# A value queue that may empty three chunks, earlier reads for endings, and shift rows begun two half steps sooner

## The chip, the cores and the metric

The kernel runs on one core of a Trainium2 chip. The metric is the device time of one execution in microseconds; the time before is the median of three runs, 5637.28 us (5630.33 to 5653.89). The profile is one more execution, taken by the hardware profiler.

## The reference

The input x has 8 batch items of 2048 tokens with 512 channels, all in float32. The layer computes

```
xn = layernorm(x)
q, k = xn @ Wq.T + bq, xn @ Wk.T + bk          # 8 heads of 8 channels
v    = xn @ Wv.T + bv                           # 8 heads of 64 channels
scores = q k^T / sqrt(8);  scores = where(scores >= 0, scores, 0.2 * scores)
s   = gamma * (softmax(scores) @ v) + xn
ffn = xn @ W.T + sum_e gate_e * (xn @ Wd_e.T @ Wu_e.T)   # 4 experts of rank 1, 2, 4, 8;
                                                # only the top gate of a token is kept
out = x + s * silu(ffn)
```

The gate is a softmax over scaled cosines between a projection of xn (Wp, bp) and `sim`.

## The kernel before

**The attention loop.** A batch item has 4 blocks of 512 tokens and 4 pairs of heads. A *sequence* is one (item b, pair p, query block n), so there are 16 sequences in an item and 128 in all; sequence s has pair s % 4 and block (s % 16) // 4 (`where`, L524). A sequence goes over the 2048 keys in 16 *chunks* of 128. The inner loop of the main program (L1030 to L1057) takes one chunk per pass; I call a pass a *half step*, as the code's helpers do, and i is its chunk. A half step issues, in this order: the shift of the current scores by their row maximum as a matmul of two rows (`less_max`, L657), the score matmuls of the next chunk (`score`, L640), one maximum unit of a later sequence (`max_unit`: matmuls mx, L586, and a VectorE maximum mxr, L597), the exponentials on ScalarE (`exp`, L669), the leaky slope of the next scores on ScalarE (`leaky`, L651), then a filler, and the addition of the exponentials on GpSimd for the denominators (`add_up`, L701, 128 x 1024 elements; none at i = 0).

**Maxima.** The softmax subtracts the true row maximum, so the maxima of a sequence are computed one sequence ahead. The unit of half step i of sequence s is number s*16 + i + 16 + LEAD, with LEAD = 9; the first 16 + LEAD units are done in the prologue. All units share one PSUM tile with one buffer (`ps_x`), so the matmuls of a unit wait for the VectorE maximum of the unit before. When the last unit of a sequence has been issued (at i = 6), `shift_rows` (L599) is put into slot 1 of a small scheduler.

**The scheduler.** There are three slots: an *ending* of a sequence, a `shift_rows`, and the background work `behind` (projections of the next item, `project_block`, and the feed-forward part of this one, `lift_block`). Each is a generator whose yields say how it may be continued. `go_on` (L810), called first in every filler, advances slots that said IDLE, so one IDLE is one half step. The filler is `half_full` (L833) for items 0 to 6 and `half_light` for the last. It either issues *values*, that is the matmuls `weigh` (av, L681) of one or two chunks waiting in the list `last`, or background matmuls, by a budget `due`. `run` counts how many chunks of values a half step may take, at most two and not past the end of a sequence; a chunk that ends a sequence and stands first is `alone`.

**shift_rows.** First half step: a reduction m (L603, VectorE). Next: big and max (L609, L610, VectorE), and six small GpSimd instructions (L611 to L616), which stand ahead of that half step's addition. After two IDLEs: a 32 x 32 transpose (L621, VectorE), four DMAs that write it to SH (L623) and four that read SH back into the tile shift (L629). All DMAs are issued by SyncE, in order.

**Ending.** The values of the last chunk put `ending` (L703) into slot 0. It copies the sums avs from PSUM (L708); in the next half step it waits until its block has been lifted, then reads gs, xs[:,0] and xs[:,1] (L714 to L717, 256 KB each: gated feed-forward, x, and xn from HBM); after three more IDLEs come the denominators (matmuls L724; VectorE L732, L734, L736), in the next half step the transposes atp (L741; VectorE L743, L744, the latter reads xs), and in the one after L747 and L748, followed by the write of the output. The tile that L741 to L748 use is in PSUM pool `ps_m`, of one buffer, as are most tiles of the background. On TensorE and VectorE all of this stands in program order with the scores and maxima.

Of the kernel before, what the change touches and what calls it, by code (L numbers as in the profile page):

```python
# [8 lines left out]
FP = mybir.dt.float32  # L9
# [12 lines left out]
NT = BLK // 128  # L22
# [10 lines left out]
def fused_layer_kernel(  # L33
# [37 lines left out]
    nc = tc.nc  # L71
    B, M, C = x.shape
    NC = C // 128
    NB = M // BLK
    CH = NB * NT
    SEQ = NPAIR * NB

    xv = x.rearrange("b (n p t) c -> b n p t c", p=128, t=NT)
# [5 lines left out]
    two = ctx.enter_context(tc.tile_pool(name="two", bufs=2))  # L84
# [12 lines left out]
    GS = [tc.dram_tile([NB, 128, NT, C], FP, name=f"GS{b}") for b in range(B)]  # L97
    XN = [tc.dram_tile([NB, 128, NT, C], FP, name=f"XN{b}") for b in range(B)]
# [145 lines left out]
    TINY, SLOW, WAIT, HOLD, FREE, IDLE = 5, 4, 3, 2, 1, 0  # L244
# [50 lines left out]
    lifted = []  # L295
# [228 lines left out]
    def where(s):  # L524
        return s // SEQ, s % NPAIR, (s % SEQ) // NPAIR
# [28 lines left out]
    def load_values(s):  # L554
        if s >= B * SEQ:
            return
        b, p, n = where(s)
        while b not in valued:
            force()
        vts[s] = two.tile([128, CH, 128], FP, name="v_sb")  # L560
        nc.sync.dma_start(out=vts[s], in_=VS[b][p])
# [37 lines left out]
    def shift_rows(s):  # L599
        if s >= B * SEQ:  # L600
            return
        m = sm.tile([128, 2 * NT, 1], FP, name="m")
        nc.vector.reduce_max(m, mxr.pop(s).rearrange("p e t n -> p (e t) n"), axis=AX.X)  # L603
        yield IDLE

        ml = sm.tile([128, 2 * NT], FP, name="ml")
        c = parts[s % 2][:, 0 : 4 * NT].rearrange("p (i m) -> p i m", i=2)
        big = sm.tile([128, 2 * NT], FP, name="big")
        nc.vector.tensor_scalar(big, m[:, :, 0], 0.0, SLOPE, ALU.min, ALU.mult)  # L609
        nc.vector.tensor_scalar_max(m[:, :, 0], m[:, :, 0], 0.0)  # L610
        nc.gpsimd.tensor_tensor(ml, m[:, :, 0], big, ALU.add)  # L611
        nc.gpsimd.tensor_tensor(big, ml, splitter.to_broadcast([128, 2 * NT]), ALU.mult)
        nc.gpsimd.tensor_tensor(ml, ml, minus_one.to_broadcast([128, 2 * NT]), ALU.mult)
        nc.gpsimd.tensor_tensor(c[:, 1, :], big, ml, ALU.subtract)
        nc.gpsimd.tensor_tensor(c[:, 0, :], big, c[:, 1, :], ALU.subtract)
        nc.gpsimd.tensor_tensor(c[:, 1, :], ml, c[:, 0, :], ALU.subtract)  # L616
        for _ in range(2):
            yield IDLE

        cT = sm.tile([128, 32], FP, name="cT")  # L620
        nc.vector.transpose(cT, parts[s % 2])  # L621
        for q in range(4):
            nc.sync.dma_start(  # L623
                out=SH[s % 2][:, :, :, q, :].rearrange("i e t j -> (i e t) j"),
                in_=cT[32 * q : 32 * q + 4 * NT, :],
            )
        shift = qp.tile([128, BLK], FR, name="shift")
        for g in range(4):
            nc.sync.dma_start(  # L629
                out=shift[STK * g : STK * g + 2, :].bitcast(FP),  # L630
                in_=SH[s % 2][:, g % 2].rearrange("i t q j -> i (t q j)"),
            )
        shifts[s] = shift
# [59 lines left out]
    def add_up(s, i, ex):  # L693
# [6 lines left out]
            acc[s] = two.tile([128, 2, BLK], FP, name="acc")  # L700
        nc.gpsimd.tensor_tensor(acc[s], old, ex, ALU.add)  # L701

    def ending(s):  # L703

        b, p, n = where(s)
        cols = slice(p * 128, (p + 1) * 128)
        avs = two.tile([128, BLK], FP, name="avs")
        nc.vector.tensor_copy(avs, avt.pop(s))  # L708
        yield IDLE
        sums = acc.pop(s)  # L710
        while (b, n) not in lifted:
            yield IDLE
        gs = two.tile([128, NT, 128], FP, name="gs")
        nc.sync.dma_start(out=gs, in_=GS[b][n][:, :, cols])  # L714
        xs = two.tile([128, 2, NT, 128], FP, name="xs")
        nc.sync.dma_start(out=xs[:, 0], in_=xv[b, n][:, :, cols])
        nc.sync.dma_start(out=xs[:, 1], in_=XN[b][n][:, :, cols])  # L717
        for _ in range(3):
            yield IDLE
        yield TINY  # L720

        dps = ps_m.tile([128, 2, NT, 32], FP, name="dps2", tag="m")
        for q in range(4):
            nc.tensor.matmul(  # L724
                dps[32 * q : 32 * q + 32],
                lhsT=ones[:, 0:32],
                rhs=sums.rearrange("p e (t q j) -> p e t q j", t=NT, q=4)[:, :, :, q, :],
                start=True,
                stop=True,
            )  # L730
        dv = dps.rearrange("p e t j -> p (e t) j")
        nc.vector.tensor_tensor(dv, dv, diag.unsqueeze(1).to_broadcast([128, 2 * NT, 32]), ALU.mult)  # L732
        rd = sm.tile([128, NT, 2, 1], FP, name="rd")
        nc.vector.reduce_sum(rd.rearrange("p t e o -> p e t o"), dps, axis=AX.X)  # L734
        rd = rd.rearrange("p t e o -> p (t e) o")
        nc.vector.reciprocal(rd, rd)  # L736
        spend(0.5)
        yield TINY
        tp = ps_m.tile([128, NT, 128], FP, name="atp", tag="m")
        for t in range(NT):  # L740
            nc.tensor.transpose(tp[:, t, :], avs[:, t * 128 : (t + 1) * 128], ident)  # L741
        tv = tp.rearrange("p t (e d) -> p (t e) d", e=2)
        nc.vector.tensor_tensor(tv, tv, rd.to_broadcast([128, NT * 2, DV]), ALU.mult)  # L743
        nc.vector.tensor_tensor(tp, tp, xs[:, 1], ALU.add)  # L744
        spend(0.5)
        yield WAIT
        nc.vector.tensor_tensor(tp, tp, gs, ALU.mult)  # L747
        nc.vector.tensor_tensor(gs, tp, xs[:, 0], ALU.add)  # L748
        nc.sync.dma_start(out=ov[b, n][:, :, cols], in_=gs)
# [5 lines left out]
    for b in range(B):  # L755
# [7 lines left out]
        t0, run = SEQ * b + LIFTED, 0.0  # L763
# [11 lines left out]
    def due_at(h):  # L775
        w, t = h * END, 0.0
        for _, _, _, cost, end in tasks:
            w += cost * max(0.0, min(1.0, (h - t) / (end - t)))
            t = end
        return w  # L780
# [44 lines left out]
    last = []  # L825
# [7 lines left out]
    def half_full():  # L833


        run = 0
        for w in last[:2]:
            run += 1
            if w[1] == CH - 1:
                break  # L840
        alone = run and last[0][1] == CH - 1
        if go_on():
            values(run)
            return
        j = (ahead() or [None])[0]
        if j == 2 and state[2] != HOLD and spent[0] > due[0] + AHEAD:
            j = None
        if j is not None and state[j] == TINY:
            values(min(run, 1))
            go(j)  # L850
            ended[0] = True
        elif j is None or len(last) > MUCH - (state[j] != HOLD) or (ended[0] and run > 1):
            ended[0] = False
            for g in stats.values():
                next(g, None)
            values(run)
        else:
            if alone:
                values(1)
            go(j)  # L860
            if state[j] == HOLD and not alone:
                go(j)
            ended[0] = state[j] != HOLD
# [15 lines left out]

    MUCH, AHEAD = 3, 6.0  # L880

    LEAD = 9
    END = 1.0
    total = B * SEQ * CH

    with tc.manual_schedule():
# [110 lines left out]
        first, late = shift_rows(0), set_up_ffn(ul)  # L997
        units = [(0, u) for u in range(CH)] + [(1, u) for u in range(LEAD)]
        for n in range(1, NB):
# [30 lines left out]
        for s in range(B * SEQ):  # L1030
            for i in range(CH):
                if i <= 3 and s + 2 not in qst and (where(s + 2)[0] in (0, *ready) or i == 3):
                    load_stacks(s + 2)
                if i >= 6 and s + 1 not in vts and (where(s + 1)[0] in valued or i == 13):
                    load_values(s + 1)
                due[0] = due_at(s + (i + 1) / CH)
                u = s * CH + i + CH + LEAD
                nxt = s * CH + i + 1


                less_max(s, i, sc0, 0)
                if nxt < total:
                    sc1 = score(nxt // CH, nxt % CH)
                max_unit(u // CH, u % CH, flip=True)
                less_max(s, i, sc0, 1)
                if u % CH == CH - 1 and u < total:
                    queue[1], state[1] = shift_rows(u // CH), IDLE
                ex = exp(sc0)
                if nxt < total:
                    leaky(sc1)  # L1050
                if s < (B - 1) * SEQ:
                    half_full()
                else:
                    half_light()
                add_up(s, i, ex)
                last.append((s, i, ex))
                sc0 = sc1  # L1057
# [47 lines left out]
```

## Time and profile before

| | |
|---|---|
| median of three runs | 5637.28 us (5630.33 to 5653.89) |
| profiled execution | 5619.18 us, its span 5617.4 us |
| TensorE / VectorE / ScalarE / GpSimd busy | 96% / 65% / 79% / 85% |
| mean granted TensorE clock | 0.968 |
| instructions | 78032 |
| big, L609 | 128 times, 51.3 us, mean 401 ns |
| GpSimd additions, L701 | 1792 times with two inputs, mean 2361 ns |

The page gives the busy time of each engine and its share of the span, then groups of instructions by line; a group line names the source line, the engine, the operation, the tiles (out <- in), the count, the busy time and mean length, then the idle time of the engine before them and who ended it. An entry `A <- B` in the waits says that engine and line A stood still until B had finished. Matmuls of float32 appear as two records each. Weight loads (PEld) overlap matmuls, so their waits count only if TensorE's matmuls (PE) stop too. The granted clock is 1 or 0.5 in this trace.

### The profile page before, as it was taken

To read this page: it belongs to the slowest core of one execution; us is meant where nothing else is said; L and a number is where in the kernel's file an instruction comes from. 1 tells how busy PE (TensorE), PEld (TensorE's weight loads), DVE (VectorE), ACT (ScalarE), POOL (GpSimd) and SP (SyncE) were. 2 spreads that over 40 slices of the span, in tenths; PEclk is the share of its full clock that TensorE was granted. 3 is DMA by queue.
4 is the path that set the end of the run, shared out by engine and by line. 5 is a ranking of instruction groups with operands and counts; after the bars stand their busy time and mean duration, and the time that the engine had idled before them with its cause. 6 is when DMAs were issued, how large, how long until landed. Compare 5 with 4: busy or idle time off the path is not lost.

```text
span 5617.4 us, 78032 instructions
## 1 busy us (share of the span) xinstructions
PE 5378.9 (96%) x26258; PEld 1999.1 (36%) x26258; DVE 3673.9 (65%) x4988; ACT 4440.7 (79%) x8627; POOL 4779.1 (85%) x2906
## 2 busy tenths in 40 slices
PE   8999999999999999999999999999999999999998
PEld 3333333333333333333333333333333333333332
DVE  5577666766676666667666666666766766645653
ACT  2788878888888878888788887888878888767777
POOL 1789988888888888888888888888888888878878
PEclk9999999999999999999999999999999999979989
DMA  5333432434324343252432434234343333322221
GB/s 197 106 112 121 128 113 88 128 106 147 104 78 142 93 146 95 76 158 91 142 92 83 147 112 130 80 111 131 107 123 99 102 120 122 100 78 78 71 63 61
DMA packets 528264, 615.38 MB, mean 110 GB/s; under 512 B 44092, under 2 KB 438332, under 8 KB 491768
## 3 DMA queue, kind: packets, MB, share of 16 engines
q1 hardware_dynamic: 527864, 610.39, 35.6%
q8 instruction: 209, 3.42, 0.3%
q14 instruction: 191, 1.56, 0.1%
HBM read 407.88 MB, written 202.38 MB: 109 GB/s over the span
## 4 chain that ended last, share of the span: by engine, by line
PE 80%; ACT 8%; DVE 7%; DMA 2%; issue 2%; SPq 1%; POOL 1%; POOLq 0%; ACTq 0%; DVEq 0%
PE av L681 28%; PE sc L657 16%; PE zps L279 9%; PE vps L279 8%; PE mx L586 7%; ACT ex L669 5%; ACT sc L651 2%; PE pps L265 2%; DVE mxr L597 2%; PE qkps L265 2%; PE dps L265 2%; PE dps L724 1%; DMA xs<-XN 1%; PE atp L741 1%; DVE gs L748 1%
## 5 line engine op out<-in xcount | busy, mean ns | idle before, releaser
L701 POOL TENSOR_TENSOR acc<-acc,ex 128x1024 f32<-128x1024 f32 x1792 | 4231.0, 2361 | 301.7 <-ACT ex L669 189.3
L597 DVE TENSOR_REDUCE mxr<-mx 128x2 f32<-128x1024 f32 x2032 | 2480.2, 1221 | 1260.0 <-PE sc L657 1018.5
L669 ACT ACTIVATE ex<-sc 128x512 f32<-128x512 f32 x4096 | 2231.0, 597 | 972.2 <-PE sc L657 829.0
L651 ACT ACTIVATE sc<-sc 128x512 f32<-128x512 f32 x4096 | 2237.7, 593 | 18.9 <-PE sc L640 18.9
L681 PE MATMUL av<-ex,v_sb 128*64 128x512 f32 x8192 | 2149.5, 630 | 11.6 <-DVE avs L708 9.2
L657 PE MATMUL sc<-shift,ones_r 2*128 2x512 f32 x4096 | 1679.7, 463 | 75.5 <-ACT sc L651 66.9
L586 PE MATMUL mx<-k,q_sb 32*128 32x512 f32 x4096 | 1445.4, 454 | 37.0 <-DVE mxr L597 35.9
L657 PEld LDWEIGHTS sc<-shift,ones_r 2*128 2x128 f32 x4096 | 703.6, 187 | 1560.4 <-ACT sc L651 1450.5
L640 PE MATMUL sc<-q_sb,k 32*128 32x512 f32 x4096 | 1037.4, 503 | 0.0
L681 PEld LDWEIGHTS av<-ex,v_sb 128*64 128x64 f32 x8192 | 469.7, 138 | 839.6 <-issue 805.2
L586 PEld LDWEIGHTS mx<-k,q_sb 32*128 32x128 f32 x4096 | 562.2, 188 | 61.2 <-DVE mxr L597 49.4
L279 PE MATMUL zps<-w_sb,xnT 128*128 128x512 f32 (+1 forms) x1120 | 541.0, 597 | 32.7 <-DMA xnT<-XT 14.1
L279 PE MATMUL vps<-wv_sb,xnT 128*128 128x512 f32 x960 | 475.2, 619 | 7.4 <-DVE gs L748 7.2
L701 POOL TENSOR_TENSOR acc<-ex 128x1024 f32<-128x1024 f32 x128 | 301.8, 2358 | 197.3 <-ACT ex L669 197.3
L640 PEld LDWEIGHTS sc<-q_sb,k 32*128 32x128 f32 x4096 | 385.9, 185 | 0.8 <-issue 0.8
L279 PEld LDWEIGHTS zps<-w_sb,xnT 128*128 128x128 f32 x1120 | 187.6, 192 | 270.3 <-issue 247.9
L279 PEld LDWEIGHTS vps<-wv_sb,xnT 128*128 128x128 f32 x960 | 164.0, 189 | 209.7 <-issue 195.9
L518 DVE SCALAR_TENSOR_TENSOR g<-th,zps 128x512 f32<-128x512 f32 x128 | 88.0, 688 | 189.2 <-ACT th L517 189.2
L611 POOL TENSOR_TENSOR ml<-m,big 128x8 f32<-128x8 f32 x128 | 26.2, 205 | 176.6 <-DVE m L610 176.6
L349 DVE TENSOR_TENSOR vb<-vps,bv_sb 128x512 f32<-128x512 f32 x120 | 83.0, 691 | 95.6 <-PE vps L279 95.4
L265 PE MATMUL dps<-xnT,wd_sb 128*128 128x512 f32 (+1 forms) x280 | 139.1, 607 | 0.0
L265 PE MATMUL pps<-xnT,wp_sb 128*128 128x512 f32 (+1 forms) x280 | 130.9, 585 | 5.0 <-DVE gs L748 5.0
(124 smaller groups left out, 2656.7 us busy)
## 6 DMA issues: line engine op xcount, KB each, us to landing
v_sb<-VS SPq DMA_DIRECT2D x127, 1024.0 KB
k<-KS SPq DMA_DIRECT2D x256, 256.0 KB
XN<-xn SPq DMA_DIRECT2D x32, 1024.0 KB
q_sb<-QS SPq DMA_DIRECT2D x256, 128.0 KB
xnT<-XT SPq DMA_DIRECT2D x32, 1024.0 KB
GS<-g SPq DMA_DIRECT2D x32, 1024.0 KB
gs<-GS SPq DMA_DIRECT2D x128, 256.0 KB
xs<-in_x_dram SPq DMA_DIRECT2D x128, 256.0 KB
```

Of the source, the lines that this page charges most:

```text
L265: nc.tensor.matmul(ps[:, part], lhsT=wt[:, c, :], rhs=xnT[c][:, part], start=(c == 0 and part.start == 0), stop=(c == NC - 1 and part.stop ...
L279: nc.tensor.matmul(ps[:, part], lhsT=xnT[c][:, t * 128 : (t + 1) * 128], rhs=wt[:, c, part], start=(c == 0 and part.start == 0), stop=(c = ...
L349: nc.vector.tensor_tensor(vb[:, :, t, :], ps.rearrange("p (h d) -> p h d", h=NPAIR), bv_sb.rearrange("p (h d) -> p h d", h=NPAIR), ALU.add,)
L518: nc.vector.scalar_tensor_tensor(g[:, t, :], th, 1.0, ps, ALU.add, ALU.mult)
L586: nc.tensor.matmul(parts[e], lhsT=q_sb[r, t * 128 : (t + 1) * 128], rhs=k_sb[r, kb // 2 * BLK : (kb // 2 + 1) * BLK], start=True, stop=True,)
L597: nc.vector.reduce_max(mxr[s][:, :, t, kb : kb + 1], mx, axis=AX.X)
L640: nc.tensor.matmul(sc[e], lhsT=k_sb[r, i // 2 * 128 : (i // 2 + 1) * 128], rhs=q_sb[r, :], start=True, stop=True,)
L651: nc.scalar.activation(sc[e], sc[e], AF.Prelu, alpha=SLOPE)
L657: nc.tensor.matmul(sc[e], lhsT=ones_r[r, :], rhs=shifts[s][r, :], start=False, stop=True, skip_group_check=True,)
L669: nc.scalar.activation(ex[:, e, :], sc[e], AF.Exp, scale=qscale)
L681: nc.tensor.matmul(avt[s][64 * e : 64 * e + DV, :], lhsT=v_sb[:, i, 64 * e : 64 * e + DV], rhs=ex[:, e, :], start=(i == 0), stop=(i == CH ...
L701: nc.gpsimd.tensor_tensor(acc[s], old, ex, ALU.add)
```

## The change

Four edits. `half_full` sets `run` to 3 when three chunks wait and the third ends a sequence. The three reads of an ending become a function, `read_for_ending`, which the main loop calls from i = 12 on for the current sequence; it does nothing if the block isn't lifted yet, and the ending then reads as before (with one more IDLE). `shift_rows` has four IDLEs in place of two between its GpSimd instructions and the transpose, and one more between the writes and the reads of SH. LEAD is 11 in place of 9, so a sequence's last unit is issued at i = 4, the prologue has 27 units in place of 25, and the transpose stays at i = 9.

```diff
@@ shift_rows
-        for _ in range(2):
+        for _ in range(4):
             yield IDLE
         cT = sm.tile([128, 32], FP, name="cT")
...
                 in_=cT[32 * q : 32 * q + 4 * NT, :],
             )
+        yield IDLE
         shift = qp.tile([128, BLK], FR, name="shift")
@@
+    reads = {}
+
+    def read_for_ending(s):
+
+        b, p, n = where(s)
+        if s >= B * SEQ or s in reads or (b, n) not in lifted:
+            return
+        cols = slice(p * 128, (p + 1) * 128)
+        gs = two.tile([128, NT, 128], FP, name="gs")
+        nc.sync.dma_start(out=gs, in_=GS[b][n][:, :, cols])
+        xs = two.tile([128, 2, NT, 128], FP, name="xs")
+        nc.sync.dma_start(out=xs[:, 0], in_=xv[b, n][:, :, cols])
+        nc.sync.dma_start(out=xs[:, 1], in_=XN[b][n][:, :, cols])
+        reads[s] = gs, xs
+
@@ ending
         sums = acc.pop(s)
-        while (b, n) not in lifted:
+        while s not in reads:
+            read_for_ending(s)
             yield IDLE
-        gs = two.tile([128, NT, 128], FP, name="gs")
-        nc.sync.dma_start(out=gs, in_=GS[b][n][:, :, cols])
-        xs = two.tile([128, 2, NT, 128], FP, name="xs")
-        nc.sync.dma_start(out=xs[:, 0], in_=xv[b, n][:, :, cols])
-        nc.sync.dma_start(out=xs[:, 1], in_=XN[b][n][:, :, cols])
+        gs, xs = reads.pop(s)
         for _ in range(3):
             yield IDLE
@@ half_full
             if w[1] == CH - 1:
                 break
+        if len(last) > 2 and last[2][1] == CH - 1:
+
+            run = 3
         alone = run and last[0][1] == CH - 1
@@ main program
-    LEAD = 9
+    LEAD = 11
@@ main loop
                     load_values(s + 1)
+                if i >= 12:
+                    read_for_ending(s)
                 due[0] = due_at(s + (i + 1) / CH)
```

## The prediction

> **What bounds it now.** I read the page first, then the waits, then the timeline around the longest waits of TensorE. On the page the engine that ends last is TensorE:
>
> ```profile
> PE 5378.9 (96%) x26258; PEld 1999.1 (36%) x26258; DVE 3673.9 (65%) x4988; ACT 4440.7 (79%) x8627; POOL 4779.1 (85%) x2906
> ...
> PE 80%; ACT 8%; DVE 7%; DMA 2%; issue 2%; SPq 1%; POOL 1%; POOLq 0%; ACTq 0%; DVEq 0%
> ```
>
> So only what TensorE issues, or what stops it, counts. From the timeline I took every half step's length (first score matmul to the next one's) and grouped the 2048 by what TensorE does in them besides scores and maxima. Undisturbed (tenth percentile) two chunks of values take 2.53 us, one chunk 2.22 (ScalarE's four passes set it), two projection matmuls 2.57, one chunk with denominators 2.24 or with an ending's transposes 2.37. These add to 5048 us of the 5466 in the loop; 417 us are lost to waits and to a halved clock. The change must earn its time there. Who causes it:
>
> ```profile
> PEld sc L657 <- ACT sc L651: 1450.5, 2143, 3.2
> ...
> POOL ml L611 <- DVE m L610: 176.6, 127, 45.2
> ...
> PE mx L586 <- DVE mxr L597: 35.9, 20, 3.7
> ...
> DVE atp L744 <- DMA xs<-XN: 25.9, 8, 4.0
> ```
>
> The columns are total, times, longest. The first line is no loss (weights waiting while matmuls run); the third and fourth are one story, as the timeline shows (start, duration, [idle, releaser]); VectorE, then TensorE:
>
> ```profile
> 2744.93 0.70 DVE L743 TENSOR_TENSOR atp<-atp,rd 128x512 f32<-128x512 f32 x1
> 2748.96 0.70 DVE L744 TENSOR_TENSOR atp<-atp,xs 128x512 f32<-128x512 f32 x1 [3.33 <-DMA xs<-XN]
> 2749.57 1.22 DVE L597 TENSOR_REDUCE mxr<-mx 128x2 f32<-128x1024 f32 x1
> ...
> 2747.37 0.50 PE L640 MATMUL sc<-q_sb,k 32*128 32x512 f32 x2
> 2750.84 0.79 PE L586 MATMUL mx<-k,q_sb 32*128 32x512 f32 x2 [2.97 <-DVE mxr L597]
> ```
>
> VectorE is in order: the ending's sum waits for xs, the maximum queues behind it, the single mx buffer is not freed, TensorE stops. In the stretch table the clock then falls to 0.50 (fields: window, length, busy per engine, clock, DMA):
>
> ```profile
> 2749.70:2756.50 6.80, 5.66 (x17) 1.77 (x17) 3.75 (x6) 1.58 (x4) 4.88 (x8) 0.50 0.18 57
> ```
>
> **Early reads of endings.** Nothing is added on SyncE: three DMAs per ending move from half steps 1 to 3 of the next sequence to half step 12 of its own. Behind them stand the next q/k loads: they land some 8 us after issue and are first used 20 us or more after it, now 15 or more, since the maxima start two half steps sooner. 0.79 MB ahead of them, at the 319 GB/s of the stretch before the stop above, is 2.5 us: covered. Seven endings, one in each batch item but the last, pay now: their reads stand behind eight key/query writes and two 1 MB writes. Their half steps took 7.41, 7.95, 8.33, 8.23, 5.95, 8.89 and 8.80 us = 55.6, against 7 x 2.53 = 17.7: 37.9 over, and the half steps after them lost 4.0 more. In the new order these reads stand ahead of those writes, by some five half steps (13 us). About 0.2 each stays (other endings of this shape): gain 41.9 - 1.4 = **40.5 us**. How much of it is clock is where a rule is to be weighed. The Trainium skill (TensorE: Matmul & The Clock Gate, "HAM oscillation") puts the rule as no idle gap above about 3.4 us. The gap above is 2.97 us and the clock halves all the same; by the rule I would count the seven waits alone, 25.7 us less some 0.8 of slack each, 20 us. I take the row, since six of the seven show the slow stretch. If the reads don't help: 0.
>
> **Shift rows: maxima earlier.** LEAD 11 puts the reduction m at i = 4 (was 6), big/max and POOL's six instructions at i = 5 (was 7); the transpose stays at i = 9 with its four writes, the four reads of shift go to i = 10. They are used at the next i = 0, six half steps (15 us) on, so a queue of one 1 MB load ahead of them is covered. The transpose waited for POOL once (3.8 us): spacing it gains about nothing. What matters is who shares VectorE's half step with m (0.19) and big/max (0.16 + 0.17). An ending brings 1.05, then 1.40, then 1.38 us, beside the maximum's 1.22, in half steps of 2.5. Laying the two programs' orders side by side: big/max share a half step with an ending's 1.4 us pair 79 times before, 43 after; m does 57 times before, never after. The others now stand mostly beside a bias add (21), a key split (14) or the gated product (13). Before the first and last VectorE idles 0.8 and 1.5 us anyway (waits of 95.4 us by 117 and 189.2 by 128); with the split big makes 1.7 us, against 1.35 of idle before the next maximum and some 0.5 until TensorE needs it. Unstretched I cost these at nothing.
>
> Batch items 1 to 6 repeat the same 16 sequences, so I went through those. Unstretched: in sequences 5, 7, 11 background matmuls wait for the ending's PSUM bank 0.85 us; m or big out of the way gives 0.2 each; 4 and 14 (1.02, 1.07 now; the new order equals that of 5) gain 0.2 each; 2 gains 0.5; 8, 10, 12 0.15 each; 1 and 15 0.1 each. Sum 2.15 per item.
>
> Stretched: big is not always 0.16 us.
>
> ```profile
> L609 DVE TENSOR_SCALAR big<-m x128: 159/161/1871, 109.4 to 5544.4; 128x8 f32<-128x8 f32 x128
> ...
> 2450.38 1.87 DVE L609 TENSOR_SCALAR big<-m 128x8 f32<-128x8 f32 x1
> ...
> 2442.53 9.69 POOL L701 TENSOR_TENSOR acc<-acc,ex 128x1024 f32<-128x1024 f32 x4
> ```
>
> The 1.87 us end at 2452.25, when POOL's addition ends (2452.22). 23 of 128 are so stretched. The Trainium skill (SBUF — State Buffer, "Who interferes with whom") explains it: such a VectorE op and a GpSimd op take a port pair in turn, for a whole instruction. That speaks against moving big: POOL is busy 85%, so the rule alone gives 128 x 0.85 x half of 2.36 = 128 us of stretching wherever big stands. The row gives 51.3 - 128 x 0.16 = 31 us, because POOL's next instruction is L611, which itself waits for big; only an addition left over from the half step before can block. At the new place, i = 5, I compared the end of that addition with the end of the maximum: late by 1.8 to 2.1 us in sequences 3, 6 and 9 of an item (POOL has just done a block's small steps), early by 0.34 to 0.47 in 0, 1, 4, 14, and by 2 in 15. So the same three are stretched. In 3 big will stand alone: the losses of 0.40 and 0.67 go, gain 1.0. In 6 it stands before a bias add: 2.05 + 0.36 + 0.69 less 1.35 of idle and 0.4 of slack is some 1.3 us of stall instead of 1.83 with a slow clock in half the cases (3.0 us for the sequence): gain 1.4. In 9 it now stands before an ending's pair: stall 2.4, where 1.85 stood: with the clock drop that follows already (2.7), no gain (between +1 and -2.5). Sum 2.4 per item; together 4.55 x 6 = **27 us**. Item 0, whose order differs, has one such stall with a slow clock (3.3 us in sequence 1): 3 us.
>
> **Third chunk.** It fires seven times, once in each of items 0 to 6, not 128 times: the queue seldom holds three. One half step of 2.53 + 0.86 = 3.39 us takes the place of lighter ones, and other steps shift. Pricing both orders by kind of half step gives +5.3 us in all (14 fewer two-chunk steps, 18 more one-chunk ones, 7 triples), +0.9 per item. Against it in sequence 3 a norm matmul's wait (0.96) and a slow clock in two of six cases (0.4) go, as three value steps now stand between; for it, 1 and 3 get a light step more beside the gate, where the clock may drop (2.5 us, a fifth of the cases each: 1.0). Net +0.5 per item: **-4 us** of the gain with item 0. Bounds: +5 gain, -25 loss (drops everywhere).
>
> **Prologue.** Two more maximum units there, two fewer at the end. 2 x 0.7 (TensorE) to 2 x 1.4 us come before the loop; the loop's fifth half step then waits 14.1 us for a DMA, which hides them; without this cover, +3 at most. The end gains 2 x 0.35 at most. I take 0.
>
> **Sum.** 40.5 + 27 + 3 - 4 = 66.5. Made against the profiled execution: span 5617.4 - 66.5 = 5550.9, with the 1.8 around it 5552.7. That execution (5619.18) is 18.1 below the median of the runs shown, 5637.28; so I predict 5637.28 - 66.5 = 5571 us.
>
> **Rivals.** (a) Only the reads pay; what m and big leave is taken by the next thing late on VectorE or by clock drops in the new light steps: 5637 - 41 = 5597. For it: most VectorE gains are 0.2 us each. (b) The reads start early but are then behind other loads, or the drop only moves: 5637 - 26 = 5611. Against: the rings carried little in the window where they now stand. (c) Slower: the port at i = 5. If POOL's leftover addition ends 0.4 us later than now, big is stretched to 1.9 us also in sequences 0, 1, 4 and 14, each before an ending's pair (1.9 + half of 2.5 for the clock = 3.1 us, 26 times = 81), and in 2, 7, 8, 10, 11, 12 before other work (0.8 us, 40 times = 32): 5571 + 113 = 5684. It decides from a lag of 0.35 us; against it, POOL skips an addition at every i = 0, and in the new order nothing of its chain stands between there and i = 5 either. (d) More: the drops in 9 and 15 (2.7 and 3.2 per item) go with the new phase: 5571 - 33 = 5538.
>
> **Chances.** Forecast 0.57, (a) 0.20, (b) 0.07, (c) 0.06, (d) 0.10. A measurement of this kernel tells about 0.5% from no change: 5609 to 5665. Forecast, (a) and (d) lie below, (b) on the edge. Faster 0.85, same 0.09, slower 0.06. Range 5535 to 5612, from (d) to (b); the forecast's own is 5552 to 5590.
>
> **What would show it.** No wait of an ending's sum for XN; the seven long half steps at 2.6 to 2.8; mean clock above 0.968 (some 0.972); L609's total still 45 to 60 us, about 20 stretched. Wrong would be: over 40 stretched, xs waits in a new place, or as many slow-clock stretches as before (40).

## The result, and the profile after

Nothing. The changed kernel takes 5635.81 us (median of 20 runs, 5608.04 to 5650.67), the kernel before in the same session 5633.18 us (20 runs, 5615.75 to 5653.89): ratio of the means 0.9997, 95% interval 0.9983 to 1.001. I had said 5571. The profiled execution after took 5636.9 us (span 5635.1, clock 0.958), about its median; the one I had worked from (5619.18) was 14 us below the median of its kernel.

The page after, the rows that answer to those of before:

```profile
PE 5421.0 (96%) x26258; PEld 2010.0 (36%) x26258; DVE 3689.4 (65%) x4990; ACT 4442.7 (79%) x8627; POOL 4777.9 (85%) x2906
...
PE 82%; DVE 7%; ACT 7%; issue 3%; DMA 1%; SPq 0%; POOL 0%; ACTq 0%; POOLq 0%; DVEq 0%
```

TensorE has the same instructions and is busy 42 us longer. That is the sign of a lower clock, not of more work. The waits after (total, times, longest):

```profile
POOL ml L611 <- DVE m L610: 134.8, 127, 45.2
...
PE mx L586 <- DVE mxr L597: 19.2, 20, 1.7
```

No wait of the ending's sum for xs is left (25.9 us before), and TensorE's waits for the maximum fell from 35.9 to 19.2 us. So the edit did to the waits what it was to do. The seven half steps that took 5.95 to 8.89 us take 2.70 to 2.72. Against that stands this row of the tile big (shortest, median and longest in ns, then when the first and last ran):

```profile
L609 DVE TENSOR_SCALAR big<-m x128: 158/160/2189, 112.7 to 5556.8; 128x8 f32<-128x8 f32 x128
```

Its longest rose from 1871 to 2189 ns and its total from 51.3 to 66.5 us; 30 of 128 are stretched for 23, among them five in sequence 4, where I had ruled it out, and sequences 3 and 9 of item 0. I compared the two traces sequence by sequence: every half step's length less its undisturbed length (the tenth percentile of its kind in both traces together), mean of items 1 to 6, in us per sequence. I call a stretch at half clock a drop.

| sequence | excess before | after | half-clock time before | after |
|---|---|---|---|---|
| 3 | 2.97 | 2.12 | 1.1 | 1.8 |
| 4 | 2.36 | 5.85 | 0 | 5.6 |
| 6 | 3.18 | 2.16 | 1.7 | 0.6 |
| 9 | 5.85 | 11.46 | 6.8 | 22.1 |
| 13 | 6.82 | 1.21 | 5.1 | 0 |
| the 11 others, sum | 22.6 | 21.5 | 9.7 | 8.6 |

Sequence 13 gave what the reads were to give, 5.6 per item. Sequences 4 and 9 took 9.1 back, and undisturbed length rose by 9.7 us in the loop. Half-clock time in the loop rose from 328 to 446 us. This is sequence 9 of item 3 in the timeline after (start, duration, [idle, releaser]); POOL, VectorE, then TensorE:

```profile
2584.99 4.82 POOL L702 TENSOR_TENSOR acc<-acc,ex 128x1024 f32<-128x1024 f32 x2
...
2587.67 2.17 DVE L609 TENSOR_SCALAR big<-m 128x8 f32<-128x8 f32 x1
2589.95 0.69 DVE L756 TENSOR_TENSOR atp<-atp,rd 128x512 f32<-128x512 f32 x1
2590.68 0.70 DVE L757 TENSOR_TENSOR atp<-atp,xs 128x512 f32<-128x512 f32 x1
2591.28 1.21 DVE L597 TENSOR_REDUCE mxr<-mx 128x2 f32<-128x1024 f32 x1
...
2592.55 0.50 PE L586 MATMUL mx<-k,q_sb 32*128 32x512 f32 x2 [1.71 <-DVE mxr L597]
```

POOL's addition ends at 2589.81, big at 2589.84. Behind it stand the ending's pair and the maximum, and TensorE waits 1.71 us for its mx buffer. It is the chain of the wait that the change removed, with big in the place of xs. The stretch table behind it (window, its length, then busy time of TensorE, its weight loads, VectorE, ScalarE and GpSimd; granted clock third from the end):

```profile
2585.00:2592.00 7.00, 5.84 (x39) 2.18 (x31) 6.58 (x11) 5.44 (x11) 6.22 (x10) 1.00 0.01 2
...
2592.00:2599.00 7.00, 6.45 (x25) 3.07 (x25) 4.54 (x8) 3.04 (x7) 6.76 (x4) 0.61 0.13 37
2599.00:2606.00 7.00, 7.00 (x23) 1.76 (x22) 4.70 (x17) 4.78 (x10) 5.79 (x3) 0.50 0.01 1
```

The clock stays halved for 13.7 us, over the gate (the choice of the expert) and the light half steps behind it, those with one chunk of values. Before, big (1.67 us) stood without an ending's pair there and the drop lasted 6.8 us.

### The profile page after: what moved, and what is told of

Same layout as the page of the kernel before. It is cut to its first block, busy times and chain, and to the rows that moved or that the text cites. A ratio compares the mean times of both kernels' runs of the same rounds, so it can differ in the third digit from the quotient of the medians.

```text
span 5635.1 us, 78208 instructions
## 1 busy us (share of the span) xinstructions
PE 5421.0 (96%) x26258; PEld 2010.0 (36%) x26258; DVE 3689.4 (65%) x4990; ACT 4442.7 (79%) x8627; POOL 4777.9 (85%) x2906
## 4 chain that ended last, share of the span: by engine, by line
PE 82%; DVE 7%; ACT 7%; issue 3%; DMA 1%; SPq 0%; POOL 0%; ACTq 0%; POOLq 0%; DVEq 0%
PE av L682 29%; PE sc L658 16%; PE zps L279 9%; PE vps L279 8%; PE mx L586 7%; ACT ex L670 5%; PE qkps L265 2%; PE pps L265 2%; ACT sc L652 2%; PE dps L265 2%; DVE mxr L597 2%; PE dps L737 1%; PE atp L754 1%; DVE atp L756 1%; PE gps L446 1%
## 5 line engine op out<-in xcount | busy, mean ns | idle before, releaser
L586 PE MATMUL mx<-k,q_sb 32*128 32x512 f32 x4096 | 1460.3, 457 | 24.4 <-DVE mxr L597 19.2
L641 PE MATMUL sc<-q_sb,k 32*128 32x512 f32 x4096 | 1048.8, 508 | 0.0
L279 PE MATMUL zps<-w_sb,xnT 128*128 128x512 f32 (+1 forms) x1120 | 560.5, 617 | 28.1 <-DVE gs L761 14.6
L611 POOL TENSOR_TENSOR ml<-m,big 128x8 f32<-128x8 f32 x128 | 26.2, 205 | 134.8 <-DVE m L610 134.8
L724 DVE COPY avs<-av 128x512 f32<-128x512 f32 x128 | 87.9, 686 | 74.0 <-PE av L682 71.9
```

Source lines behind the costliest of these rows:

```text
L279: nc.tensor.matmul(ps[:, part], lhsT=xnT[c][:, t * 128 : (t + 1) * 128], rhs=wt[:, c, part], start=(c == 0 and part.start == 0), stop=(c = ...
L586: nc.tensor.matmul(parts[e], lhsT=q_sb[r, t * 128 : (t + 1) * 128], rhs=k_sb[r, kb // 2 * BLK : (kb // 2 + 1) * BLK], start=True, stop=True,)
L641: nc.tensor.matmul(sc[e], lhsT=k_sb[r, i // 2 * 128 : (i // 2 + 1) * 128], rhs=q_sb[r, :], start=True, stop=True,)
```

## The experiments

In short: the early reads gain; the moved maxima gain elsewhere but make a longer drop in sequence 9; the third chunk takes back what the two gain together. Runs with the stretch of big taken away, and with light half steps filled, show where the losses sit.

All ratios are to the kernel before on the same chip, with their 95% intervals; differences in us are taken from the ratios. "Equal clock" is a line of time against mean granted clock through a kernel's runs, read at 0.964, where the kernel before takes 5635 us and the changed kernel 5610; the slope is some 3300 to 5000 us per unit of clock, the correlation 0.83 or more in size. With four to seven runs for many kernels such a reading is rough.

### Each edit alone

The early reads alone: the function `read_for_ending`, its call at i = 12 and the new loop in `ending`, nothing else.

> The kernel before with the early reads alone (LEAD 9, no third chunk, two IDLEs). Theory A (the reads pay what the traces show, some 40 us, and the other edits give it back): ratio 0.993, about 5594 us; seven half steps of sequence 13 at 2.6 to 2.8 us, no wait for XN. Theory B (the reads only move the clock's drops elsewhere): ratio 0.998 to 1.001, the half-clock time of the loop unchanged at some 330 us.

0.9955 (0.993 to 0.9981), 25 us. At equal clock 27 us: the waits are gone, but the mean clock (0.963) is that of before (0.9635). In the profile the drops of sequence 13 are gone, and those of sequence 15 last 30.7 us in four items, where they had lasted 10.2 at most. So there is a good part of theory A, and some of theory B.

The third chunk alone:

```diff
+        if len(last) > 2 and last[2][1] == CH - 1:
+            run = 3
```

> The kernel before with the third chunk of values alone. Theory A (the third chunk costs little: the order it makes adds some 5 us of undisturbed half steps): ratio 1.000 to 1.002. Theory C (it is the third chunk's new order, and not the earlier maxima, that costs what the reads gain): ratio 1.004 or more, with the clock's drops of sequences 4 and 9 in this kernel.

1.002 (1.0005 to 1.0034), 11 us slower: the top of theory A's range, short of theory C's. More on its wider effect stands below.

The moved maxima alone:

```diff
-        for _ in range(2):
+        for _ in range(4):
...
+        yield IDLE
         shift = qp.tile([128, BLK], FR, name="shift")
...
-    LEAD = 9
+    LEAD = 11
```

> The kernel before with the earlier maxima and the wider spacing alone (LEAD 11, the three IDLEs). Theory A (big, stretched before an ending's pair in sequences 4 and 9, stops TensorE and halves its clock there): ratio 1.004 to 1.007, some 25 to 40 us, L609 stretched some 30 times, sequence 9 longer by 4 to 6 us in each item. Theory C (the earlier maxima do no harm without the third chunk): ratio 0.995 to 1.000. My prediction on record had 0.995 for this edit.

0.9992 (0.9979 to 1.0005): 4 us, at the upper end of theory C's range. But the profile shows both theories at work: sequence 3 is 1.3 us and sequence 6 1.4 us shorter per item, sequence 9 is 6.0 us longer. The 4 to 6 us of theory A in sequence 9 are there, and the gains elsewhere pay for them: at equal clock this kernel is 17 us faster, and its mean clock is 0.960 for 0.9635.

### Pairs of edits

> The changed kernel without the third chunk. In the traces big is stretched in sequence 4 of five of six items in the changed kernel, and once where the shift rows are moved without the third chunk. Theory A' (the third chunk delays POOL there, and adds 9 us of undisturbed half steps): 20 to 30 us under the changed kernel, ratio to before 0.9945 to 0.9965, one or no stretched big in sequence 4. If the third chunk only costs what it did alone: 11 us, ratio 0.9975 to 0.9985.

0.9914 (0.9891 to 0.9938), 48 us: the edit without the third chunk is a clear gain, larger than I expected. Against it the changed kernel is 0.84% slower, 47 us, plus or minus 15 (intervals taken as independent). The third chunk costs that here.

> The changed kernel with the maxima where they were (LEAD 9, two IDLEs, none between the writes and reads of SH). Theory A' (shift rows moved harm beside the third chunk, gain a little without it): reads -28 us and third +11 us, ratio 0.9965 to 0.9975, that is 15 us under the changed kernel. If the earlier maxima gain what I predicted (27 us): 5655 us or more, ratio 1.003 or more.

1.0054 (1.0031 to 1.0076), 30 us slower than before. I had expected 15 us under the changed kernel; it is 32 above it. So the maxima's new place does gain what I predicted in this company, and it is again the third chunk that costs: 60 us, plus or minus 16, on top of the early reads (0.9948, the mean of their two measurements). The mean clock is the lowest of all kernels, 0.955. At equal clock the third chunk costs 27 us here, 20 in the changed kernel and 16 alone; the rest is clock.

Why so much from an edit that fires seven times? The profile of early reads with moved maxima (no third chunk) against that of the changed kernel: 62.7 us in the loop, 19.7 in item 0, 38.1 in items 1 to 6, 4.9 in item 7. In items 1 to 6, sequence 4 has 22.2 of it, undisturbed length 8.8 (in sequence 0, where the third chunk fires in these items), sequences 9 and 15 some 4 each. In item 0 sequence 9 has 11.6 and sequence 3 3.7: the third chunk brings item 0, whose order had differed, into the pattern of the others, with big stretched there too. In sequence 4 POOL tells the rest. Without the third chunk, item 3 (POOL, then VectorE):

```profile
2337.08 7.26 POOL L702 TENSOR_TENSOR acc<-acc,ex 128x1024 f32<-128x1024 f32 x3
...
2344.55 0.16 DVE L609 TENSOR_SCALAR big<-m 128x8 f32<-128x8 f32 x1
2345.00 0.20 POOL L611 TENSOR_TENSOR ml<-m,big 128x8 f32<-128x8 f32 x1 [0.65 <-DVE m L610]
...
2357.03 0.20 POOL L309 TENSOR_TENSOR rstd<-mv,ln_eps 128x4 f32<-128x4 f32 x1 [0.79 <-DVE mv L305]
```

With it:

```profile
2349.03 0.20 POOL L309 TENSOR_TENSOR rstd<-mv,ln_eps 128x4 f32<-128x4 f32 x1
...
2350.84 16.98 POOL L702 TENSOR_TENSOR acc<-acc,ex 128x1024 f32<-128x1024 f32 x7
2367.77 2.38 POOL L702 TENSOR_TENSOR acc<-ex 128x1024 f32<-128x1024 f32 x1
2370.23 7.24 POOL L702 TENSOR_TENSOR acc<-acc,ex 128x1024 f32<-128x1024 f32 x3
...
2375.95 1.55 DVE L609 TENSOR_SCALAR big<-m 128x8 f32<-128x8 f32 x1
...
2380.22 0.50 PE L586 MATMUL mx<-k,q_sb 32*128 32x512 f32 x2 [1.05 <-DVE mxr L597]
2381.55 3.49 PE L279 MATMUL zps<-w_sb,xnT 128*128 128x512 f32 x4 [0.60 <-DVE gs L761]
```

In both, big starts 17.3 to 17.4 us after the sequence does. Without the third chunk POOL is free 0.21 us earlier, with it 1.52 us later. What delays POOL is the norm of a later block (L309 to L313, 1.8 us of POOL). The third chunk runs the background's order ahead, and the norm's POOL steps move from half step 11 of sequence 4, after big, to half step 11 of sequence 3, before it. Up to there POOL is no later with the third chunk: its addition starts 0.26 us after that half step does, for 0.55 without. Of the five half steps behind it three take 2.22 us, less than an addition of 2.36, and POOL is still late when big starts.

This accounts for 17 of the 22.2 us: 3.1 in each of four items and 4.6 in a fifth. The other 5.4 are item 2's, where big isn't stretched in sequence 4. There a drop of 23.9 us begins at half step 12 of sequence 3 and runs into sequence 4. The kernels with the third chunk and the maxima unmoved have no stretched big in sequence 4 at all, and such a drop in two of six items each. This is the one of item 4 in the pair above (clock third from the end):

```profile
3040.90:3064.80 23.90, 23.56 (x70) 7.45 (x72) 11.89 (x22) 13.64 (x27) 17.13 (x8) 0.50 0.36 110
```

Half steps 12 and 13 of sequence 3 take one chunk of values there, where they took two; with 14, 15 and the next sequence's first that makes five light ones behind the gate. In items 1 to 6 these drops cost sequences 3 and 4 together some 8.8 us each. So the third chunk has two ways to cost more than its longer half steps: POOL's delay where the maxima have moved, and a long drop where light half steps line up. Which share of the 60 us each has isn't shown: of the 47 us between that profile and that of the early reads alone, 21 lie in item 7, where the third chunk never fires.

### Without the stretch

The two VectorE operations on the maxima, and POOL's sum of them, are replaced by one activation on ScalarE:

```diff
-        nc.vector.tensor_scalar(big, m[:, :, 0], 0.0, SLOPE, ALU.min, ALU.mult)
-        nc.vector.tensor_scalar_max(m[:, :, 0], m[:, :, 0], 0.0)
-        nc.gpsimd.tensor_tensor(ml, m[:, :, 0], big, ALU.add)
+        nc.scalar.activation(ml, m[:, :, 0], AF.Prelu, alpha=SLOPE)
```

In the changed kernel:

> The changed kernel with the two small VectorE operations on the row maxima and POOL's sum of them replaced by one leaky-slope activation on ScalarE, so that no VectorE operation waits for GpSimd there. Theory A (the stretch of big and the stops behind it cost what the reads gain): ratio to before 0.989 to 0.993, sequences 4 and 9 back to before or below. Theory C (the order costs it, not the stretch): ratio 0.998 to 1.002, sequence 9 still at 46 us or more.

0.9875 (0.9845 to 0.9904), more than I expected. 69 us of the changed kernel's time hung on these operations; mean clock 0.967, sequence 9 back to 41.8 us. The activation also takes away POOL's sum and its wait for VectorE (134.8 us in the changed kernel, though POOL is 0% of the chain that ended last), so this run alone doesn't single out the stretch. Only in the two places that the trace named:

```diff
+        if s % SEQ in (5, 10):
+            nc.scalar.activation(ml, m[:, :, 0], AF.Prelu, alpha=SLOPE)
+        else:
```

> The changed kernel, with the leaky slope of the row maxima on ScalarE only where shift_rows runs in sequences 4 and 9 of an item; in the other 14 big stays on VectorE. Theory A' (the loss sits at these two places: big stretched before an ending's pair, then a long clock drop): most of the 67 us of the repair everywhere, ratio to before 0.988 to 0.992, the drops of sequence 9 at 8 us or less per item. If the repair's gain is spread over all sequences, or is a matter of less work on VectorE and POOL: two sixteenths of it, ratio 0.998 to 1.000.

0.9894 (0.9875 to 0.9913): 58 of the 69 us come from 2 of 16 sequences. It is the places, not the amount of work. Sequence 9 of item 3 in this kernel (VectorE, ScalarE, TensorE):

```profile
2571.89 0.22 ACT L610 ACTIVATE ml<-m 128x8 f32<-128x8 f32 x1
2571.93 0.70 DVE L759 TENSOR_TENSOR atp<-atp,rd 128x512 f32<-128x512 f32 x1 [0.16 <-PE atp L757]
2572.66 0.70 DVE L760 TENSOR_TENSOR atp<-atp,xs 128x512 f32<-128x512 f32 x1
...
2574.54 0.54 PE L586 MATMUL mx<-k,q_sb 32*128 32x512 f32 x2
```

No 2 us stand before the pair, the mx matmul has no wait, and the granted clock is 1.00 in the 21 us around it. Of the six drops of sequence 9 in items 1 to 6 two are left, of 20.5 and 13.7 us. In the kernel with early reads and moved maxima, sequence 9's place alone (`s % SEQ == 10`):

> Early reads and moved maxima (no third chunk), with the leaky slope on ScalarE for the one shift_rows of an item that runs in sequence 9. Theory A' (sequence 9 lost 5 to 6 us per item to the stretched big and its long drop): some 30 us under the kernel with reads and moved maxima alone (0.9914), ratio 0.985 to 0.988. If sequence 9's drop comes anyway: 0.990 to 0.992.

0.987 (0.9845 to 0.9895), 25 us (plus or minus 19) under 0.9914, as theory A' said. With the activation everywhere, the kernel before:

> The kernel before with the leaky slope of the row maxima on ScalarE in place of two VectorE operations and one of POOL (LEAD 9, nothing else of the change). Theory A (stretched big costs the kernel before too: 31 us of VectorE time, stops and drops in sequences 6 and 9): ratio 0.994 to 0.997. Rival (the stretch only costs at the new place): ratio 0.999 to 1.001.

0.9928 (0.9908 to 0.9947): 41 us, more than I expected; the stretch had cost the kernel before as well. With early reads, the maxima unmoved:

> Early reads with the leaky slope on ScalarE everywhere and the maxima left where they were (LEAD 9, two IDLEs), no third chunk. Theory A' (moving the maxima only matters through the port): the same as with the maxima moved, 0.983 to 0.985. If moving m and the pair off the ending's half steps gains what I predicted without the stretch (2.15 us per item, 13 us): 0.9855 to 0.987.

0.9863 (0.9841 to 0.9884), in the range for moves that gain without the stretch. With early reads and moved maxima, no third chunk:

> The changed kernel without the third chunk and without the stretched pair (the maxima's leaky slope on ScalarE). Theory A: 0.9875 of the changed kernel so repaired, less the 0.2 to 0.3% that the third chunk costs: ratio 0.984 to 0.986. If the third chunk's cost was the stretch's too: 0.987 to 0.988.

0.9834 (0.9811 to 0.9856), 5546.0 us. So moving the maxima, freed of the stretch, gains 0.29% or 16 us, plus or minus 18: the 13 us of my unstretched sum fit, and so does nothing. The third chunk without any stretch still costs 0.41%, 23 us, plus or minus 21.

### Filling the light half steps

Half steps with one chunk of values use TensorE least. The next three kernels were to add matmuls of zeros there, and their condition could never come true (their traces have no such matmul), so they are repeats of before, of the changed kernel and of the early reads.

> The kernel before with two more matmuls in each light half step of items 0 to 6 (one chunk of values or none, no background): they multiply 64 columns of zeros with keys and add the zeros to the open sums, so the result is unchanged. Theory K (the clock halves where a short stop meets light half steps, because TensorE is then used for less than about half of a few microseconds): the drops that begin in sequences 0, 1, 3, 9 and 15 go, half-clock time in the loop falls from some 330 (of which about 150 in the last item, which gets no such matmuls) to 190 to 220 us, ratio 0.988 to 0.992. Theory L (the clock follows something else, heat or a schedule of its own): the drops stay, ratio 1.000 to 1.005.

> The changed kernel with the same two zero matmuls in its light half steps. Theory K: the half-clock time of sequences 9, 15, 3, 0 goes (some 250 us of the items 0 to 6 in the profiled run), ratio to before 0.980 to 0.985; against the kernel before with the same matmuls 0.991 to 0.996, since the waits that the change takes away (26 us by reading the times at an equal clock) then show. Theory L: ratio 0.999 to 1.004, as the changed kernel alone.

> The early reads alone, with the zero matmuls in light half steps. Theory K: here the drop of sequence 13 goes with the reads and comes back nowhere, so the difference to the kernel before with the same matmuls is my prediction's 40 us (0.7%), where without them it was 20 to 25; ratio to before 0.981 to 0.985. If the reads save their waits alone: 26 us under that kernel.

1.0003 (0.9991 to 1.0016), 1.0003 (0.9989 to 1.0017), and 0.9941 (0.9919 to 0.9964). They tell nothing of theory K; the last is a second measurement of the early reads, 33 us. With the condition mended, and matmuls that use all rows and columns:

```diff
+        if spent[0] - begun < 0.4 and n - len(last) == 1 and w[1] < CH - 1:
+            for _ in range(2):
+                nc.tensor.matmul(avt[w[0]], lhsT=zero_r, rhs=kst[s % 3][:, 0:BLK],
+                    start=False, stop=False, skip_group_check=True)
```

> In the kernels of the call before, the zero matmuls were never issued (their condition could not come true), so those were repeats of before, after and the early reads alone. Here they are: two per light half step (one chunk of values, no background), of 128 rows by 128 columns, 192 in all in items 0 to 6; they add zeros to the open sums. In the traces so far the clock's drops part best from the rest by the share of TensorE's cells that matmuls use in the 3.4 us before (matmul time x rows x columns / 128 / 128): drops at most 0.24, all but half a per cent of other windows above that; the two add some 0.19 to a light half step. Theory K (the drops come of short stops beside light half steps): drops of sequences 0, 1, 3, 9, 15 go, half-clock time in the loop 190 to 240 us for 328, ratio 0.988 to 0.993. Theory L (they follow something else): ratio 1.000 to 1.005.

1.0012 (0.9992 to 1.0033), in theory L's range. In the trace theory K was half right: of six drops in sequence 15 of items 1 to 6 one is left, and the mean clock rose from 0.964 to 0.969. But sequence 13's drops and five of six in sequence 9 stay, behind stops of TensorE (1.64 us in sequence 9 of item 2), and at equal clock the matmuls cost 31 us.

> The changed kernel with the same zero matmuls, 128 x 128, in its light half steps. Theory K: its long drops in sequences 9, 15, 3 and 0 go; half-clock time in the loop 190 to 240 us for 447; ratio to before 0.981 to 0.986, and against the kernel before so filled 0.992 to 0.996, because the waits that the change takes away (26 us at an equal clock) then show. Theory L: as the changed kernel, 1.000.

0.9952 (0.9932 to 0.9973), 0.6% under the kernel before so filled. That is less than I said, but now the changed kernel does gain.

> The early reads alone, with the 128 x 128 zero matmuls. Theory K: the drop of sequence 13 goes and comes back nowhere, so it is 35 to 42 us (0.993) faster than the kernel before so filled: the 40.5 us of my prediction; ratio to before 0.981 to 0.986. If the reads save their waits alone: 26 us under that kernel (0.9955).

0.9898 (0.9878 to 0.9917), clock 0.975: 1.1% under the kernel before so filled, 64 us, plus or minus 16, more than the 35 to 42 expected, though against before it falls short of the 0.981 to 0.986 I had named. The 192 matmuls of zeros take 74.7 us in this trace. With the light half steps filled, the early reads get their part of the clock. Why they get more I can't say.

> The fastest kernel so far (early reads, maxima moved, leaky slope on ScalarE, no third chunk) with the 128 x 128 zero matmuls in light half steps. If what is left of the drops costs more than the matmuls do (they cost 30 us at an equal clock, and took 9 us' worth of clock off most in the early reads): ratio 0.982 to 0.984, no better; if the drops go nearly all: 0.977 to 0.981.

0.9827 (0.9808 to 0.9846), 5542.6 us, not to be told from 0.9834. Without the stretch the matmuls cost what they bring. This kernel and the one without them are the fastest.

## Why the prediction was wrong

**The step that failed is the third chunk.** I put it at "-4 us" with a bound of -25. It costs 47 us, plus or minus 15, in the changed kernel and 60 on top of the early reads. I priced kinds of half steps (my +5.3 us measured 9.3 between the profiles with and without it) and single drops (2.5 us in a fifth of the cases, where a drop beside the gate lasts 23.9 us and costs some 8.8). I did not follow POOL through the new order. The sentence that fell is "4 and 14 ... gain 0.2 each", on a lag that said POOL was early by 0.34 to 0.47 in sequence 4. I had looked only for POOL's chain between i = 0 and i = 5; it moved to five half steps ahead of i = 0, and POOL carries a delay through short half steps. This is rival (c), which I had given 0.06, with its price of 3.1 us per place right in four of five items (4.6 in the fifth) and its places wrong: it decided in sequence 4 and in item 0, not in 0, 1 and 14. The stretch is not the whole of it: with the activation on ScalarE the third chunk still costs 23 us, plus or minus 21, and on top of the early reads it costs 60 though big in sequence 4 is never stretched there.

**Sequence 9.** "No gain (between +1 and -2.5)" per item; the moved maxima alone lost 6.0 in the profile, and repairing the place gained 25 us, plus or minus 19. The stop came, somewhat shorter than I said (1.71 us for 2.4). The clock did not do what I said: I counted one drop of the old length, and the drop, now ahead of the gate and the light half steps, lasts 13.7 to 30.7 us instead of 6.8.

**Moved maxima.** Predicted 30 us. Measured 4 alone, 19 on top of the early reads (0.9914 to 0.9948), 32 on top of reads and third chunk. Sequences 3 and 6 gave 1.3 and 1.4 for my 1.0 and 1.4. What misses is sequence 9.

**Early reads.** Predicted 40.5. Measured 25 and 33 alone, 44 beside the moved maxima (0.9914 to 0.9992), 37 beside the activation on ScalarE (0.9863 to 0.9928). The mechanism held: no wait for XN, 2.70 to 2.72 us for 2.6 to 2.8. The clock part, which I took from the row and against the Trainium skill's rule (TensorE: Matmul & The Clock Gate, "HAM oscillation": no idle gap above some 3.4 us), is real where it stood: with the 2.97 us wait gone the drop of sequence 13 is gone, and the 1.71 us of sequence 9 are followed by one. But alone the mean clock did not rise, because drops elsewhere got longer. The only exception is the pair with the third chunk, which is slower than the third chunk alone by 0.3%; there the clock fell from 0.9645 to 0.955 and at equal clock the reads gain 16 us. Why the drops get so long in that order is open.

**Prologue.** The loop starts at 132.1 for 129.9 us, 2.2 us later. But its fifth half step, the one that waits for a DMA, takes 12.7 for 18.8 us, and the first sequence ends at 188.5 for 188.2. The cover held, and 0 was about right.

**The sum.** Reads and moved maxima together gave 48 us (35 to 61), where I had 70.5, so 22 us were missing there, about what the repair of sequence 9 brought (25, plus or minus 19); the third chunk took 47, all that was left. Of my signs, "mean clock above 0.968" failed (0.958), "45 to 60 us" for L609 failed (66.5), "about 20 stretched" failed (30). They failed together, and they name the stretch and the clock, though not the third chunk behind them. A sign of being wrong came true too: as many drops as before (41 in both traces).

## What to carry to other kernels

An edit that changes how much a filler takes moves every later step of every engine, so price it by following the second busiest engine's queue through the new order, and by looking where light steps line up, not by counting kinds of steps. A VectorE operation that can be held by GpSimd is dangerous where large VectorE work stands behind it; three tiny operations put on a third engine were worth 41 us without any reordering. And when a wait is removed, look where the clock's next drop begins before the drop's cost is counted as gained.

## What the runs showed of the hardware

The clock does not follow idle time alone. A wait of 1.71 us halves it in sequence 9 after, with TensorE busy 5.8 of the 7 us before. In the kernel before, sequence 13 of item 4 has nearly the wait that halved the clock in item 3 (2.97 us, above), and there the clock stayed whole (the wait, then the stretch table as above):

```profile
3430.31 0.50 PE L586 MATMUL mx<-k,q_sb 32*128 32x512 f32 x2 [2.92 <-DVE mxr L597]
...
3425.00:3432.00 7.00, 4.08 (x22) 1.42 (x22) 3.65 (x8) 3.51 (x7) 2.25 (x6) 1.00 0.71 231
```

In the traces of all 20 kernels, after the prologue, I took for every drop (611) the 3.4 us before it. The share of TensorE's cells in use there is an estimate: each matmul record counts rows x columns / 128 / 128 of the array, for the time that such records take in these traces. That is 0.84 ns for each of the 512 columns that a float32 record streams (429 ns from one record of the value projection to the next), and 0.64 ns for scores, maxima, shifts and zeros (326 ns between the two records of a maximum). The share was at most 0.41 in 90% of the drops and 0.45 in all. Of 29261 other windows at full clock 0.1% lie below 0.41, and their median is 0.75. Time with any matmul in flight, counted so, parts them less well: 1.0% of the other windows lie below the drops' 90% mark. (The 0.24 of an expectation above comes from counting about half the time for a column.) Score and maximum matmuls use 32 of the 128 rows and count a quarter, so that a TensorE that is "96% busy" can still come near this mark. It is a correlation, no run sets the mark itself, and the filled kernels, which add time and cells together, can't tell the two measures apart.

A drop that begins ahead of light half steps lasts through them: 30.7 us in sequence 15 of four items in the early reads alone, where filled none in sequence 15 lasts over 17.1. A light half step at half the clock takes 3.06 us, for 2.22 at the whole, so it works through fewer columns per us. By the same count the half-clock windows after which the clock stayed halved had a share of 0.37 in the median (90% below 0.43), the last ones 0.42 (90% above 0.38): about the level at which drops begin. What ends a drop isn't shown beyond that.

In both places shown the stretched big ends 0.03 us after POOL's addition (2589.84 for 2589.81, 2377.50 for 2377.47); with POOL free it takes 0.16 us.
